# One more slot on the seven-product scheme, wider row maxima and a reordered list in a quantised GLU kernel

## The chip, the core and the metric

The kernel runs on one core of a Trainium2 chip. The metric is the device time of one execution in microseconds. The core's engines run side by side, each through its own list of instructions in order, and wait for each other on semaphores: TensorE (PE: matrix products into PSUM; PEld is its weight load), VectorE (DVE), ScalarE (ACT), GpSimd (POOL) and SyncE (SP), whose queue issues nearly all DMA transfers here. An instruction that waits holds up everything behind it on its engine or queue.

## The reference

Inputs are x (4 batches of 1024 tokens, 512 wide), a condition vector of 128 for each batch, and three weight matrices. Cut to what matters:

```python
scale = cond @ norm_w.T + 1.0
h = x * (scale[:, None, :] * rsqrt(mean(x * x) + EPS))
u = h @ up_w.T                        # 512 -> 4096
val, gate = split(u, 2)               # 2048 each
h = val * gelu(gate)
hq = round(h * 127 / max|h| per token) / (127 / max|h| per token)
wq = sign-like rounding of down_w by its mean magnitude
y = hq @ wq.T + x                     # 2048 -> 512
```

All four batches share the weights. The first projection is made in parts of fp16 (a high part and what is left of it), three matmul terms for each product, so that it holds fp32 accuracy.

## The kernel before

The 2048 columns of val and of gate are cut into NJ = 16 groups of 128, called slots; a global slot number g is batch times 16 plus j. A batch's 1024 tokens are two halves of 512. So a slot is a 2 by 2 arrangement of blocks (gate and val, each for two token halves), with the width of 512 split in two halves as well.

A slot can be made in two ways.

- *Plain* (function `plain`, matmuls at L705): four blocks, `gate.j.h` and `value.j.h` for h = 0, 1, each of twelve matmuls of 128x512 (four parts of the width, three terms). ACT then takes a gelu (`gelu.j.h`, L751) and DVE multiplies value and gelu (`out.j.h`, L761).
- *Seven products* (class `Slot`, matmuls at L690): a scheme of Strassen's kind over the 2 by 2 blocks. Seven products of six matmuls each are added up in three PSUM banks, with copies from bank to bank by ACT (L797, L805, L812), two gelus (L819, L836) and four DVE steps (L825, L833, L842, L845). Its operands are sums and differences of the weight blocks and of the token blocks.

Batches 1 to 3 make all slots by seven products, from weight sums that the first batch has spilled to DRAM (`s_spill`, L462) and that are loaded back (`s_load`, L476 and L478). In the first batch the weights themselves are still being read, scaled to powers of two, split, summed and transposed while PE works. There slots 0 to FAST - 1 are plain and slots FAST to 15 are made by seven products; FAST is NJ - 2 = 14.

What a slot j of the first batch needs, by the names of its steps: `w_load` (the two weight rows, 512 KB, L299), `w_range` (ACT, L315), `w_factor` (small DVE steps, L325 to L335), `w_scale` (ACT, L365), `rows_high` and `rows_low` (ACT L391, DVE L395: the high and low halves in fp16), `rows_turn` (a DMA transpose, L399, into the slot's place); and for the sums `s_sum` (four additions on POOL or DVE, L429), `s_high` (ACT, L446), `s_low` (POOL or DVE, L450) and `s_spill`. A slot on seven products in this batch also has its sums transposed on the spot by `s_turn` (two DMA transposes, L468) from `s_rows`, a pair of buffers that the next such slot uses again; its `rows_turn` moves three blocks out of four. The transposed weights lie in three places in turn (j modulo 3): two halves of SXY and an area of R. Batch 1's first slot, g = 16, uses the half of SXY that slot 13 had, and slot 17 that of slot 15.

The token side of batch 1 is made ready during batch 0 too: `t_load`, `t_square`, `t_root`, `t_scale`, `t_sum`, `t_high`, `t_low` and `t_turn` (a DMA transpose of 28 blocks, L665) for each of four groups of tokens. The quantised second weight is fetched and rounded by `d_fetch`, `d_round` and `d_sign`.

Row maxima for the quantisation: `pair_max` reduces a pair of neighbouring slots (128x1024 into 128x512, absolute maximum, L896; L891 for the first pair, straight into the result) and then combines the result with the maximum so far (L898). Step `max.i.h.n` is part n of the pair that begins at slot 2i. Pair 7 is left to batch 1.

The order of all these steps is written out by hand in `FIRST_BATCH`, one list for all engines: `take` calls each step in turn, and each puts its instructions at the end of its engine's list. In a step name the last number of `s_sum.j.n.1`, `s_low.j.n.1` and `t_sum.a.n.1` puts it on DVE; without it the step goes to POOL. `slot.g.k` is step k of a seven-product slot: 0, 2, 4, 6, 8, 10 and 13 are its products, 1, 3, 5, 7 and 12 are on ACT, 9, 11, 14 and 15 on DVE. PSUM banks are used in turn: a plain `value` uses one of two banks, which the `out` two values earlier must have read, and a `gate` one that a `gelu` must have read.

Of the kernel before, what the change touches and what calls it, by code (L numbers as in the profile page):

```python
# [51 lines left out]
def glu_quant_kernel(  # L52
# [90 lines left out]
    FAST = NJ - 2  # L143
# [742 lines left out]
    def pair_max(b, i, h):  # L886

        v = h_slots(b * NJ + 2 * i, 2)[:, :, h].rearrange("p j t -> p t j")
        m = m_view(b, h)
# [4 lines left out]
        def largest():
            gm.append(wpool.tile([P, TOK], F32, name=f"gm_{b}_{i}_{h}", tag="gm", bufs=1))
            DVE.tensor_reduce(gm[0], v, AX.X, ALU.max, apply_absolute_value=True)  # L896

        return [largest, lambda: DVE.tensor_tensor(m, m, gm[0], ALU.max)]  # L898
# [451 lines left out]
    def take(steps):  # L1350
# [15 lines left out]
        d_sum.7 c_range s_spill.1.0 rows_high.4 s_sum.2.3 d_load.1 s_spill.2.1 value.2.1 w_scale.5.0
        w_gain.2 o_sum.1 gelu.2.0 out.2.0 o_high.1 rows_low.4 rows_turn.4 gelu.2.1 gate.3.0 rows_high.5
        o_low.1 s_high.2.0 o_sum.2 s_high.2.1 value.3.0 o_sum.3 o_high.2 w_load.6 o_high.3 rows_low.5
        rows_turn.5 gelu.3.0 gate.3.1 out.2.1 d_sum.2 o_low.3 d_sum.3 max.0.0.0 s_spill.3.1 t_square.0.1
        value.3.1 d_sum.0 o_low.2 w_range.6 t_root.0 s_low.2.0.1 s_spill.2.0 c_spread d_sum.1 c_rows  # L1370
        gate.4.0 w_load.7 w_factor.6 s_sum.3.0 s_spill.4.1 w_scale.6.0 out.3.0 w_load.11 o_high.0 s_low.2.1
        s_spill.2.2 s_sum.3.1.1 w_scale.6.1 o_low.0 value.4.0 gelu.3.1 rows_high.6 out.3.1 s_sum.3.2.1
        s_sum.3.3 w_range.7 max.1.0.0 gate.4.1 w_load.8 s_high.3.1 rows_low.6 rows_turn.6 gelu.4.0
        s_high.3.0 s_low.3.0 c_copy s_low.3.1.1 w_factor.7 w_scale.7.1 value.4.1 max.0.1.0 w_scale.7.0
        t_load.1 out.4.0 s_sum.4.0 rows_high.7 rows_low.7 rows_turn.7 gelu.4.1 gate.5.0 w_range.8
        s_sum.4.1.1 d_total s_sum.4.2.1 s_sum.4.3.1 out.4.1 value.5.0 s_high.4.0 s_low.4.0 w_factor.8
        c_store w_scale.8.1 c_load c_undo w_scale.8.0 w_gain.6 d_spread gelu.5.0 s_sum.5.1.1 gate.5.1
        max.1.0.1 rows_high.8 s_sum.5.0.1 s_spill.5.1 s_sum.5.2.1 s_spill.3.2 w_range.9 out.5.0 s_spill.6.1
        rows_low.8 s_spill.3.0 value.5.1 s_spill.7.1 s_high.4.1 s_low.4.1 s_high.5.0 rows_turn.8 max.1.1.0
        gelu.5.1 c_bring max.1.1.1 gate.6.0 s_low.5.0.1 s_sum.6.1 s_sum.5.3.1 s_high.5.1 s_spill.5.0  # L1380
        w_factor.9 s_low.5.1 value.6.0 d_mean w_scale.9.1 s_sum.6.0.1 w_scale.9.0 t_scale.0.1 w_gain.8
        out.5.1 t_high.0.1 rows_high.9 t_sum.0.0.1 t_scale.0.0 gate.6.1 s_sum.6.2.1 t_high.0.0 t_sum.0.1
        max.2.0.0 gelu.6.0 s_spill.8.1 s_sum.6.3 s_high.6.0 t_low.0.0 w_range.10 value.6.1 rows_low.9
        rows_turn.9 gelu.6.1 t_sum.0.2.1 w_factor.10 w_scale.10.1 t_sum.0.3 s_low.6.0.1 gate.7.0 t_high.0.2
        t_low.0.1 out.6.0 w_scale.10.0 t_low.0.2 rows_high.10 s_spill.4.0 s_spill.5.2 value.7.0 s_sum.7.1.1
# [5 lines left out]
        w_scale.11.1 gate.8.1 gelu.8.0 s_spill.7.0 s_sum.9.0.1 out.7.1 s_sum.9.2.1 s_sum.9.1.1 s_high.9.0
        value.8.1 s_sum.9.3.1 w_load.12 t_sum.1.0.1 s_low.9.0.1 s_spill.8.2 rows_high.11 w_range.12
        rows_low.11 rows_turn.11 gate.9.0 max.3.0.1 out.8.0 t_scale.1.0 s_spill.9.0 value.9.0 gelu.8.1
        t_sum.1.1 t_load.2 gelu.9.0 w_factor.12 s_spill.11.1 out.8.1 w_scale.12.1 w_scale.12.0 s_sum.10.0.1
        t_sum.1.2.1 s_high.9.1 s_sum.10.1.1 gate.9.1 rows_high.12 t_sum.1.3 max.3.1.0 s_spill.7.2 s_low.9.1
        t_high.1.2 s_sum.10.2.1 max.3.1.1 t_high.1.1 s_high.10.0 s_sum.10.3.1 w_load.13 value.9.1
        rows_low.12 t_high.1.0 rows_turn.12 s_high.10.1 t_low.1.1 t_low.1.0 gelu.9.1 t_low.1.2 w_range.13
        gate.10.0 out.9.0 s_low.10.0.1 s_sum.11.0 t_turn.1 gelu.10.0 max.4.0.0 value.10.0 s_low.10.1 out.9.1
        s_spill.10.1 s_sum.11.2.1 s_sum.11.1.1 s_high.11.0 gate.10.1 max.4.0.1 s_sum.11.3.1 t_square.2.1
        s_low.11.0.1 s_sum.12.0 s_spill.12.1 s_high.11.1 w_load.14 gelu.10.1 w_factor.13 s_spill.11.0  # L1400
# [413 lines left out]
```

## Time and profile before

| what | us |
|---|---|
| median of 3 runs (723.93 to 724.92) | 723.95 |
| the profiled execution | 724.24 |
| its span, first to last instruction | 722.5 |
| PE busy | 716.2 |
| DVE busy | 584.4 |
| ACT busy | 420.0 |
| POOL busy | 139.4 |

A row of the profile in order of time has the start, the duration, the engine, the source line, the operation, the tile written and the tiles read, the shape and the number of merged instructions; brackets at its end hold the idle time before it and what released it. A grouped row has the count, then the busy time and the mean duration in ns, then the idle time before and its releasers. SPq stands for the queue of SP: its duration is the issuing of a transfer, not its landing.

### The profile page before, as it was taken

What the parts mean: (1) busy time and instruction counts of PE and PEld (TensorE: products, weight loads), DVE (VectorE), ACT (ScalarE), POOL (GpSimd) and SP (SyncE); (2) the same over time, 40 slices, a digit from 0 to 9 for tenths busy, and PEclk for the clock granted to TensorE, in tenths of its full rate; (3) what the DMA queues carried; (4) which work ended last, traced back from release to release, by engine and by line L of the source; (5) the groups of instructions that cost most, each with busy time, mean ns of one, the idle gap of its engine ahead of it and who ended that gap; (6) DMA issues with size and microseconds to landing.
All of it is one profiled execution on the core that took longest, in us unless ns stands there. A gap on an engine that the chain in (4) does not pass through costs nothing.

```text
span 722.5 us, 10223 instructions
## 1 busy us (share of the span) xinstructions
PE 716.2 (99%) x3676; PEld 360.7 (50%) x3676; DVE 584.4 (81%) x876; ACT 420.0 (58%) x697; POOL 139.4 (19%) x143
## 2 busy tenths in 40 slices
PE   8999999999999999999999999999999999999998
PEld 4544444444444446665444445665444444445854
DVE  7888799784898899787689887677678888755896
ACT  6898776765667774553335676544433665333473
POOL 1634331322100124440100030360020000000120
PEclk9999999999999999999999999999999999999999
DMA  7799889989995765877845646765965455453253
GB/s 276 258 290 266 236 199 254 288 185 243 281 205 117 132 157 130 210 169 176 167 101 103 131 102 184 189 162 160 216 93 111 101 103 101 102 100 98 103 172 121
DMA packets 228405, 122.64 MB, mean 170 GB/s; under 512 B 189801, under 2 KB 199805, under 8 KB 228354
## 3 DMA queue, kind: packets, MB, share of 16 engines
q1 hardware_dynamic: 228202, 121.85, 69.1%
q8 instruction: 29, 0.48, 0.3%
q14 instruction: 22, 0.18, 0.1%
q10 hardware_dynamic: 152, 0.13, 0.1%
HBM read 53.50 MB, written 23.09 MB: 106 GB/s over the span
## 4 chain that ended last, share of the span: by engine, by line
PE 96%; DVE 2%; DMA 1%; ACT 1%; SPq 0%; issue 0%
PE A L690 34%; PE E L690 17%; PE pg L705 10%; PE pv L705 10%; PE po L1052 9%; PE B L690 9%; PE po_end L1004 4%; DMA SXY<-s_rows 1%; PE pz L1169 1%; DVE gm L896 1%; PE ptx L1153 1%; PE pv L776 0%; PE po_B L1052 0%; DVE R L898 0%; PE pg L776 0%; DVE R L891 0%
## 5 line engine op out<-in xcount | busy, mean ns | idle before, releaser
L690 PEld LDWEIGHTS <-SXY 128*128 128x128 f16 x2058 | 201.2, 98 | 236.5 <-DMA SXY<-s_rows 0.7
L690 PE MATMUL A<-R,SXY 128*128 128x512 f16 x1158 | 267.4, 379 | 0.0
L690 PE MATMUL E<-R,SXY 128*128 128x512 f16 x582 | 141.4, 379 | 0.1
L825 DVE SCALAR_TENSOR_TENSOR H<-A,sg,t 128x512 f32<-128x512 f32 x50 | 37.5, 750 | 72.6 <-PE A L690 72.4
L976 DVE TENSOR_TENSOR H<-H,am 128x1024 f32<-128x1024 f32 x64 | 76.1, 1214 | 0.0
L836 ACT ACTIVATE t<-t,sg 128x512 f32<-128x512 f32 x50 | 36.0, 721 | 64.8 <-DVE t L833 64.7
L690 PE MATMUL B<-R,SXY 128*128 128x512 f16 x294 | 71.4, 379 | 0.0
L896 DVE TENSOR_REDUCE gm<-H 128x512 f32<-128x1024 f32 x56 | 69.1, 1233 | 0.9
L705 PEld LDWEIGHTS <-SXY 128*128 128x128 f16 x438 | 42.8, 98 | 51.6 <-DVE SXY L417 0.4
L912 POOL PARTITION_ALL_REDUCE am<-R x8 | 14.4, 1795 | 229.4 <-DVE R L898 229.4
L819 ACT ACTIVATE t<-B,sg 128x512 f32<-128x512 f32 x50 | 34.4, 688 | 38.3 <-PE B L690 38.3
L1052 PE MATMUL po<-wd,R 128*128 128x256 fp8e4 x416 | 52.4, 273 | 0.0
L705 PE MATMUL pg<-R,SXY 128*128 128x512 f16 x228 | 52.4, 379 | 0.0
L812 ACT COPY t<-A 128x512 f32<-128x512 f32 x50 | 29.0, 581 | 35.5 <-PE A L690 35.2
L705 PE MATMUL pv<-R,SXY 128*128 128x512 f16 x210 | 48.9, 379 | 0.0
L1052 PEld LDWEIGHTS <-R 128*128 128x128 bf16 (+1 forms) x448 | 43.8, 98 | 8.9
L805 ACT COPY v<-E 128x512 f32<-128x512 f32 x50 | 29.3, 586 | 31.6 <-PE E L690 28.0
L797 ACT COPY B<-A 128x512 f32<-128x512 f32 x50 | 28.6, 572 | 30.5 <-PE A L690 29.9
L845 DVE SCALAR_TENSOR_TENSOR H<-v,sg,t 128x512 f32<-128x512 f32 x50 | 38.8, 776 | 7.6 <-ACT t L836 7.6
L984 ACT ACTIVATE H<-H 128x1024 f32<-128x1024 f32 x38 | 39.9, 1050 | 5.2 <-DVE H L976 5.2
L842 DVE TENSOR_TENSOR v<-A,v 128x512 f32<-128x512 f32 x50 | 34.1, 683 | 10.7 <-PE A L690 9.6
L898 DVE TENSOR_TENSOR R<-R,gm 128x512 f32<-128x512 f32 x56 | 40.6, 725 | 1.0
(237 smaller groups left out, 932.5 us busy)
## 6 DMA issues: line engine op xcount, KB each, us to landing
SXY<-s_dram SPq DMA_DIRECT2D x48, 256.0 KB, 3.2
H<-in_L_cond_up_w_dram SPq DMA_DIRECT2D x13, 512.0 KB, 5.0
s_dram<-SXY SPq DMA_DIRECT2D x17, 384.0 KB, 3.2
SXY<-s_dram SPq DMA_DIRECT2D x48, 128.0 KB, 3.3
xr<-in_x_dram SPq DMA_DIRECT2D x19, 256.0 KB, 3.2
out_dram<-xr SPq DMA_DIRECT2D x19, 256.0 KB, 2.8
H<-in_x_dram SPq DMA_DIRECT2D x8, 512.0 KB, 5.8
R<-in_L_cond_down_w_dram SPq DMA_DIRECT2D x8, 512.0 KB, 6.7
```

Source lines behind the costliest of these rows:

```text
L690: PE.matmul(o, s[:, w, k, :], operand(g // NJ, c, l, k), start=start and n == 0, stop=stop and n == len(TERMS) - 1, skip_group_check=True,)
L705: PE.matmul(ps, a[k // 2][:, w, k % 2, :], XP[:, l, k, h * TOK : (h + 1) * TOK], start=n == 0, stop=n == len(terms) - 1,)
L819: ACT.activation(self.t1, self.B, AF.Gelu, scale=gain(self.g, 1))
L825: DVE.scalar_tensor_tensor(h_half(self.g, 0), self.A, gain(self.g, 0), self.t1, ALU.mult, ALU.mult)
L836: ACT.activation(self.t2, self.t2, AF.Gelu, scale=gain(self.g, 1))
L842: DVE.tensor_tensor(self.v, self.A, self.v, ALU.add)
L845: DVE.scalar_tensor_tensor(h_half(self.g, 1), self.v, gain(self.g, 0), self.t2, ALU.mult, ALU.mult)
L896: DVE.tensor_reduce(gm[0], v, AX.X, ALU.max, apply_absolute_value=True)
L898: return [largest, lambda: DVE.tensor_tensor(m, m, gm[0], ALU.max)]
L976: DVE.tensor_tensor(v, v, r.to_broadcast([P, 2, TOK]), ALU.mult)
L984: ACT.activation(v, v, AF.Copy, bias=MAGIC)
L1052: PE.matmul(po, w[:, j], m, start=start and j == 0, stop=stop and j == n - 1, skip_group_check=True,)
```

## The change

FAST goes from 14 to 13, so slot 13 of the first batch is made by seven products; `pair_max` takes a number of slots, and the first batch reduces slots 0 to 3, 4 to 7 and 8 to 11 at once (the steps `max.1`, `max.3` and `max.5` go) and the pair 12, 13 as before; the list is reordered from its first line on. In that list nine additions (six `s_sum`, three `t_sum`) and one of the `s_low` go from POOL to DVE. The diff, with the list cut to its end:

```diff
-    FAST = NJ - 2
+    FAST = NJ - 3
...
-    def pair_max(b, i, h):
-
-        v = h_slots(b * NJ + 2 * i, 2)[:, :, h].rearrange("p j t -> p t j")
+    def pair_max(b, i, h, n=2):
+
+        v = h_slots(b * NJ + 2 * i, n)[:, :, h].rearrange("p j t -> p t j")
...
     def lm(i, h, n):
         if n == 0:
-            made["m", i, h] = pair_max(0, i, h)
+            made["m", i, h] = pair_max(0, i, h, 2 if i == 6 else 4)
...
     FIRST_BATCH = """
...
-        s_high.15.0 s_low.15.0 t_sum.3.0.1 s_turn.14.1 t_sum.3.2.1 t_sum.3.3.1 s_spill.13.1 t_high.3.2
-        t_low.3.2 value.13.1 s_spill.15.1 gelu.13.1 gelu.13.0 s_turn.15.0 s_sum.15.3 out.13.0 slot.14.0
-        slot.14.1 t_low.3.1 s_spill.14.2 s_sum.15.1 slot.14.2 t_low.3.0 t_turn.3 max.5.0.1 out.13.1
-        slot.14.4 gains slot.14.6 slot.14.5 s_high.15.1 s_low.15.1 slot.14.3 slot.14.13 slot.14.14 slot.14.7
-        d_fetch.1 slot.15.0 slot.15.1 s_spill.15.0 s_load.16.0 s_turn.15.1 slot.15.2 s_load.16.1 slot.15.6
-        slot.15.7 d_fetch.2 slot.14.8 slot.14.9 d_fetch.3 s_spill.15.2 s_load.16.2 d_round.1 s_load.17.0
-        slot.15.4 s_spill.12.2 max.5.1.0 slot.14.10 slot.15.5 d_sign.0 max.5.1.1 slot.15.13 s_load.17.1
-        slot.14.11 d_sign.1 slot.14.12 slot.14.15 slot.15.3 s_spill.14.1 max.6.0.0 d_fetch.5 s_load.16.3
-        slot.15.14 max.6.0.1 d_fetch.4 s_spill.13.2 max.6.1.0 max.6.1.1
...
+        s_sum.13.2.1 gelu.11.1 out.11.1 t_root.3 rows_high.14 gate.12.0 s_high.13.0 out.11.0 w_gain.14
+        s_high.12.1 s_low.13.0 s_low.12.1.1 w_load.15 s_turn.13.0 value.12.0 s_sum.13.3.1 s_sum.14.0.1
+        s_high.13.1 max.4.0.0 gelu.12.0 s_low.13.1 gate.12.1 s_sum.14.1 s_turn.13.1 rows_low.14 w_range.15
+        s_spill.13.0 s_sum.14.2 s_spill.13.2 d_fetch.0 value.12.1 w_factor.15 rows_turn.14 gelu.12.1
+        out.12.0 w_scale.15.0 t_scale.3.0 s_high.14.0 s_low.14.0 s_turn.14.0 s_sum.15.0.1 slot.13.0
+        w_scale.15.1 slot.13.2 slot.13.1 s_sum.14.3 rows_high.15 t_scale.3.1 slot.13.4 s_high.14.1
+        s_spill.11.2 t_high.3.0 s_low.14.1.1 s_spill.14.2 slot.13.6 t_sum.3.1.1 slot.13.5 out.12.1
+        s_spill.14.0 d_round.0 s_turn.14.1 t_sum.3.0.1 slot.13.13 gains rows_low.15 slot.13.7 rows_turn.15
+        w_gain.15 s_sum.15.1.1 slot.14.0 slot.13.3 s_sum.15.2.1 t_low.3.0 slot.14.1 s_sum.15.3 slot.13.14
+        slot.14.2 t_sum.3.2.1 s_spill.13.1 s_high.15.0 s_low.15.0.1 t_sum.3.3 t_high.3.1 slot.14.6
+        s_high.15.1 s_low.15.1 t_high.3.2 t_low.3.1 s_spill.15.0 s_turn.15.0 slot.13.8 t_low.3.2 s_turn.15.1
+        slot.14.4 slot.13.9 d_fetch.1 slot.13.10 slot.14.5 t_turn.3 slot.14.3 slot.14.7 slot.14.13
+        slot.13.11 max.4.0.1 slot.15.0 slot.15.1 slot.14.14 max.4.1.0 slot.15.2 s_load.16.0 d_sign.0
+        s_load.16.1 slot.15.6 slot.15.7 s_spill.15.1 slot.14.8 slot.14.9 d_fetch.2 s_spill.15.2 slot.13.12
+        d_fetch.3 slot.15.4 d_round.1 slot.13.15 slot.14.10 slot.15.5 s_load.16.3 slot.15.3 d_sign.1
+        slot.15.13 slot.14.11 s_load.17.0 slot.15.14 slot.14.12 slot.14.15 max.4.1.1 s_load.17.1 max.6.0.0
+        s_load.16.2 max.6.0.1 s_spill.14.1 d_fetch.5 max.6.1.0 max.6.1.1 d_fetch.4 s_spill.12.2
     """
```

Earlier in the list, what the prediction speaks of stands so before and after:

```diff
-        s_high.1.0 s_low.0.1.1 s_spill.0.0 s_sum.1.3 gate.2.0 w_factor.4 w_range.5 w_load.10 out.0.1
-        rows_turn.3 w_scale.4.1 w_factor.5 s_high.1.1 out.1.1 value.2.0 d_sum.5 s_low.1.1 w_scale.5.1
...
-        gate.8.0 out.7.0 max.3.0.0 s_spill.6.0 w_scale.11.0 s_spill.6.2 value.8.0 s_spill.9.1 w_gain.10
...
+        gelu.1.1 value.1.1 s_sum.1.0.1 s_sum.1.2.1 s_high.0.1 out.1.1 t_square.0.0 s_low.0.1 s_spill.0.0
+        w_range.5 s_sum.1.3 d_load.0 gate.2.0 d_sum.5 o_sum.0 d_sum.6 s_sum.1.1.1 w_load.10 out.0.1
+        s_high.1.0 value.2.0 rows_turn.3 c_largest w_factor.4 d_sum.7 w_factor.5 w_gain.2 s_high.1.1
...
+        rows_turn.10 out.7.0 gate.8.0 s_sum.8.0.1 max.2.0.0 gelu.7.1 s_sum.8.1 s_spill.6.0 s_spill.7.0
+        value.8.0 s_spill.6.2 s_sum.8.2.1 s_high.8.0 out.7.1 s_sum.8.3.1 w_scale.11.1 s_low.8.0.1
```

More of the change, by code (lines that the diff above doesn't have):

```diff
@@ L1366, in glu_quant_kernel @@
[L1366 to L1385, printed above, removed]
@@ L1391, in glu_quant_kernel @@
[L1391 to L1400, printed above, removed]
@@ new lines, in glu_quant_kernel @@
+        s_low.1.0.1 w_scale.4.0 c_over w_scale.4.1 gate.2.1 s_sum.2.1.1 s_sum.2.0.1 w_scale.5.1 s_low.1.1.1
+        s_spill.1.0 o_sum.1 rows_high.4 d_load.1 s_spill.2.1 w_scale.5.0 s_sum.2.2.1 rows_low.4 rows_turn.4
+        value.2.1 o_high.1 s_sum.2.3 c_range gelu.2.0 o_high.3 out.2.0 gate.3.0 s_high.2.1 d_sum.2 o_sum.2
+        rows_high.5 o_sum.3 w_gain.4 gelu.2.1 value.3.0 o_low.1 d_sum.3 w_load.6 out.2.1 s_high.2.0
+        rows_low.5 rows_turn.5 gelu.3.0 gate.3.1 o_high.2 o_low.3 d_sum.0 o_low.2 w_range.6 w_load.11
@@ new lines, in glu_quant_kernel @@
+        s_spill.8.0 s_high.8.1 gate.8.1 s_low.8.1.1 t_scale.1.0 s_spill.8.2 s_sum.9.0.1 s_spill.9.1
+        s_sum.9.1.1 s_sum.9.2.1 s_high.9.0 s_low.9.0 t_sum.1.0.1 s_sum.9.3.1 w_load.12 value.8.1
+        rows_high.11 rows_low.11 rows_turn.11 gelu.8.0 gelu.8.1 w_range.12 gate.9.0 max.2.0.1 out.8.0
+        out.8.1 s_high.9.1 t_sum.1.1.1 t_load.2 value.9.0 s_sum.10.1.1 s_spill.9.0 w_factor.12 s_spill.11.1
+        s_sum.10.0.1 w_scale.12.0 t_sum.1.2.1 gelu.9.0 max.2.1.0 t_sum.1.3 w_scale.12.1 s_low.9.1 gate.9.1
@@ new lines, in glu_quant_kernel @@
+        t_high.1.1 rows_high.12 s_sum.10.2 s_spill.7.2 max.2.1.1 s_high.10.0 s_sum.10.3.1 w_load.13
+        t_high.1.2 rows_low.12 value.9.1 s_spill.9.2 t_high.1.0 rows_turn.12 out.9.0 gelu.9.1 t_low.1.1
+        s_high.10.1 s_low.10.1 t_low.1.0 gate.10.0 t_low.1.2 t_square.2.1 out.9.1 t_turn.1 s_low.10.0.1
+        t_square.2.0 value.10.0 gelu.10.0 t_root.2 s_sum.11.0.1 w_range.13 s_sum.11.2.1 s_sum.11.1
+        s_high.11.0 gate.10.1 w_factor.13 s_sum.11.3 s_low.11.0.1 w_gain.12 w_load.14 w_scale.13.0
@@ new lines, in glu_quant_kernel @@
+        s_spill.11.0 s_sum.12.0.1 t_scale.2.1 s_spill.12.1 value.10.1 gelu.10.1 s_spill.10.1 t_sum.2.0.1
+        t_load.3 w_scale.13.1 t_scale.2.0 s_spill.10.0 rows_high.13 t_sum.2.1.1 out.10.0 s_high.11.1
+        w_range.14 gate.11.0 s_sum.12.1.1 s_low.11.1 t_sum.2.2.1 t_sum.2.3.1 rows_low.13 rows_turn.13
+        t_high.2.0 value.11.0 s_sum.12.2.1 t_high.2.2 out.10.1 t_high.2.1 s_high.12.0 s_low.12.0 t_low.2.1
+        w_factor.14 gelu.11.0 t_low.2.0 gate.11.1 w_scale.14.1 s_spill.12.0 w_scale.14.0 s_spill.10.2
```

50 lines of the change are left out of this document (25 added, 25 removed).

## The prediction

> **What bounds the kernel now.** I read the page first, then busy time by stretches, then PE in order of time, then what held PE, and last the neighbours (DVE, ACT, POOL, the DMA queue of SP) at those places.
>
> ```profile
> span 722.5 us, 10223 instructions
> ...
> PE 716.2 (99%) x3676; PEld 360.7 (50%) x3676; DVE 584.4 (81%) x876; ACT 420.0 (58%) x697; POOL 139.4 (19%) x143
> ...
> 0.00:20.00 20.00, 17.30 (x85) 9.38 (x86) 16.17 (x77) 13.23 (x30) 4.12 (x9) 1.00 0.74 255
> ...
> 60.00:80.00 20.00, 20.00 (x96) 9.24 (x94) 14.27 (x32) 16.26 (x31) 6.62 (x7) 1.00 0.91 230
> 80.00:100.00 20.00, 20.00 (x94) 8.98 (x92) 19.83 (x36) 15.14 (x32) 5.40 (x7) 1.00 0.83 224
> 100.00:120.00 20.00, 20.00 (x93) 8.99 (x92) 18.95 (x36) 13.53 (x25) 7.41 (x10) 1.00 0.97 250
> ...
> 160.00:180.00 20.00, 19.76 (x93) 8.84 (x91) 9.79 (x15) 11.25 (x17) 5.05 (x5) 1.00 1.07 247
> ...
> 700.00:723.00 23.00, 19.21 (x105) 10.09 (x103) 16.60 (x24) 10.30 (x10) 0.00 (x0) 1.00 0.46 157
> ```
>
> The columns behind each stretch are PE, PEld, DVE, ACT and POOL, then the granted clock, the DMA share and GB/s. PE is busy for all but 6.3 us of the span, and nearly all of that lies in the first 20 us (2.70) and the last 23 (3.79), which the change does not touch. So the time is the number of matmuls times their pitch, plus short waits. The clock is 1.00 throughout. DVE is a near second in the first batch: 38.8 of the 40 us from 80 to 120.
>
> ```profile
> 83.33 2.75 PE L705 MATMUL pv<-R,SXY 128*128 128x512 f16 x12
> 85.99 2.75 PE L705 MATMUL pg<-R,SXY 128*128 128x512 f16 x12
> ...
> 98.94 2.75 PE L705 MATMUL pv<-R,SXY 128*128 128x512 f16 x12
> 101.68 2.75 PE L705 MATMUL pg<-R 128*128 128x512 f16 x12
> 104.38 2.75 PE L705 MATMUL pv<-R 128*128 128x512 f16 x12
> ...
> 161.35 2.75 PE L705 MATMUL pv<-R,SXY 128*128 128x512 f16 x12
> 163.94 1.46 PE L690 MATMUL A<-R 128*128 128x512 f16 x6
> ...
> 176.90 1.46 PE L690 MATMUL E<-R 128*128 128x512 f16 x6
> 178.59 1.47 PE L690 MATMUL A<-wd,SXY 128*128 128x512 f16 x6 [0.24 <-DMA SXY<-s_rows]
> 179.90 1.46 PE L690 MATMUL A<-R,SXY 128*128 128x512 f16 x6
> ```
>
> Starts tell more than durations, whose ends are modelled. Twelve matmuls take 163.94 - 161.35 = 2.59 us, so one takes 0.216 us and a product of six 1.295. Against this pitch PE loses 0.07 (85.99), 0.15 (101.68), 0.11 (104.38) and 0.395 us (178.59, due at 178.195): 0.725 us of waits in the first batch.
>
> ```profile
> 96.41 0.73 DVE L761 SCALAR_TENSOR_TENSOR H<-g,sg,pv 128x512 f32<-128x512 f32 x1
> ...
> 100.95 0.68 ACT L751 ACTIVATE g<-pg,sg 128x512 f32<-128x512 f32 x1
> ...
> 103.59 0.74 DVE L761 SCALAR_TENSOR_TENSOR H<-g,sg,pv 128x512 f32<-128x512 f32 x1
> ...
> 166.69 4.17 SPq L665 DMA_TRANSPOSE R<-nx  x1
> ...
> 172.69 5.85 DMA SXY<-s_rows
> ```
>
> The wait at 101.68 ends with ACT's gelu.7.0 (100.95 + 0.68), which frees the bank of gate.8.0; the one at 104.38 with DVE's out.7.0 (103.59 + 0.74), which frees that of value.8.0. The one at 178.59 ends when s_turn.15.1 lands (the last row is from the chain); it was issued only at 172.69, because t_turn.3 held SP's queue for 4.17 us and three more transfers stood in between. The out at 96.41 is out.6.1, used below.
>
> **The change, part by part.** Its own sum is made on the profiled execution: 724.24 us (span 722.5 and 1.74 around it), 0.29 above the median of 723.95; what is gained there I take off the median.
>
> *Products.* Slot 13 of batch 0 loses 4 plain blocks of 12 matmuls and gets 7 products of 6: 48 becomes 42, and the built programs differ by six matmuls. On the path: 6 x 0.216 = -1.295 us. Nothing else of PE changes.
>
> *The tail of the list.* s_turn.15.1 moves ahead of d_fetch.1, t_turn.3 and s_load.16.0. Between its place and slot.15.13, which needs it, stood 5 products (6.5 us); now there are 9 (11.7 us). It took 5.85 us, so the 0.395 us goes: -0.395. What is late next is t_turn.3, all of whose output slot 16's first product reads: 8 products follow its place (10.4 us) where 10 did (13.0).
>
> ```profile
> R<-nx SPq DMA_TRANSPOSE x8, 6.6
> ...
> SXY<-H SPq DMA_TRANSPOSE x9, 4.4
> ...
> s_dram<-s_rows SPq DMA_DIRECT2D x4, 256.0 KB, 3.6
> ...
> 43.45 2.33 SPq L399 DMA_TRANSPOSE SXY<-H  x1
> ...
> 49.01 1.24 PE L705 MATMUL pg<-R,SXY 128*128 128x512 f16 x5
> ```
>
> With 6.6 us to land it has 3.8 to spare: 0. If the queue ahead (s_turn.15.1, d_fetch.1) holds it for more, each us is PE's. s_load.16.1 keeps its 5 products of lead. Slot 13's own two transposes are listed 9.1 and 7.8 us ahead of need, against 4.4 for a longer one: 0. The smaller row transposes of slots 14 and 15 keep 6.5 and 9.1 us (10.4 and 11.7 before): 0. s_rows has two buffers, so s_high.14.0 waits on ACT for the spill of slot 13 (3.6 us to land); behind it stands slot 13's first copy, which PE wants two products later. Between 0 and about 1 us on ACT; I take 0 on PE.
>
> *The early list.* All other moves are in the same plan of PE; I compare leads. Row transposes of slots 4 to 13 stand 13 us or more ahead of their gates, that of slot 2 as far as before (5.2). Only one shrinks to where it could matter: rows_turn.3, whose place moves from 7.9 to 5.3 us ahead of gate.3.0. It was in fact issued at 43.45, held by the landing of s_spill.0.0, with 5.56 us to gate.3.0 at 49.01: 1.2 above the median landing. It still stands behind that spill; d_load.0 (512 KB, formerly ahead of the spill) now stands between. Bytes ahead are the same: 0; at worst the 2.1 us that 512 KB takes at 250 GB/s (the stretch 100 to 120 above), less 1.2: +0.9. At best the earlier spill gives nothing, since PE does not wait there.
>
> *DVE, ACT and POOL.*
>
> ```profile
> L896 DVE TENSOR_REDUCE gm<-H 128x512 f32<-128x1024 f32 x12 | 14.8, 1231 | 0.1
> L395 DVE TENSOR_TENSOR H<-H 128x1024 f16<-128x1024 f32 x12 | 14.6, 1218 | 2.3 <-ACT H L391 2.2
> ...
> L898 DVE TENSOR_TENSOR R<-R,gm 128x512 f32<-128x512 f32 x12 | 8.2, 684 | 0.1
> ...
> L450 DVE TENSOR_TENSOR SXY<-H,SXY 128x768 f16<-128x768 f32 x6 | 6.4, 1061 | 0.2 <-ACT SXY L446 0.2
> ...
> L395 DVE TENSOR_TENSOR H<-H 128x768 f16<-128x768 f32 x2 | 1.9, 951 | 0.0
> ...
> L429 DVE TENSOR_TENSOR H<-H x39: 405/416/779, 33.1 to 159.4; 128x256 f32<-128x256 f32 x39
> L429 POOL TENSOR_TENSOR H<-H x25: 724/732/1713, 20.4 to 165.0; 128x256 f32<-128x256 f32 x25
> ...
> L761 DVE SCALAR_TENSOR_TENSOR H<-g,sg,pv 128x512 f32<-128x512 f32 x23 | 17.0, 738 | 1.8 <-PE pv L705 1.3 <-ACT g L751 0.4
> ...
> L842 DVE TENSOR_TENSOR v<-A,v 128x512 f32<-128x512 f32 x2 | 1.4, 686 | 2.7 <-PE A L690 2.7
> ...
> L751 ACT ACTIVATE g<-pg,sg 128x512 f32<-128x512 f32 x27 | 18.1, 680 | 5.3 <-PE pg L705 5.1
> ...
> L797 ACT COPY B<-A 128x512 f32<-128x512 f32 x3 | 1.7, 570 | 3.5 <-PE A L690 3.5
> ```
>
> A maximum over four slots is not in the trace. Its ends are one two-slot reduce (1.23) and two (2.46); L395's two sizes give (1.218 - 0.951)/256 = 1.04 ns per element, so 1.23 + 1024 x 1.04 ns = 2.30, near the upper end. Fourteen reduces and twelve combinations become six of 2.30, two of 1.23 and six combinations: -12 x 1.231 - 6 x 0.684 + 6 x 2.30 = -5.1 us of DVE.
>
> [...]
>
> Back come six s_sum and three t_sum moved from POOL (9 x 0.42 = +3.8), one s_low from POOL (+1.0), slot 13's four results, two like L842 and two like L761, for two outs (+1.4), and 0.27 less for its rows: +0.8 us net in the 158 us of the batch. ACT gets three copies (0.57) and two gelus for two gelus: +1.7. POOL loses ten instructions of 0.73 us and more. None of this is on PE's path by itself; what covers it is the lead of each out, which frees a bank for PE. I summed DVE's list up to each out with these durations, less 0.08 us by which neighbours overlap. Ahead of out.6.1 it grows by 2.0 us, of out.7.0 (where PE waited) by 0.0, of out.7.1 by -0.6, of out.8.0 by 1.2, of out.9.0 by -0.9. Where DVE had idle time earlier (5.7 us from 60 to 80) the 2.0 can go; so I leave the small waits as they are: 0, ends -0.33 (all gone) and +2.0.
>
> *Sum:* -1.295 - 0.395 = -1.69; 723.95 - 1.69 = 722.26, by the profiled execution 722.55. I predict 722.3.
>
> **Rivals.**
> 1. *Only the matmuls are won.* t_turn.3 or a slot 13 transpose takes the place of s_turn.15.1 as PE's last wait, of about the same size. For it: DMA share 1.07 in 160 to 180 and two transposes more. Against: 3.8 us to spare. -1.295: 722.65.
> 2. *All waits go.* Shorter maxima and an emptier POOL let DVE reach out.7.0 in time: -1.295 - 0.725 = -2.02, 721.93. For it: L429 on DVE takes 779 ns at worst against 416, when POOL is at work. Against: DVE's list there is no shorter. [...]
> 3. *Slower: DVE falls behind between 75 and 130 us.* The first batch's DVE is full there; a four-slot reduce in front of an out holds it 1.1 us longer than a two-slot one, the list has 2.0 us more ahead of out.6.1, and value.7.1 started 1.8 us after that out had ended (98.94 against 97.14). Every us of lag that no idle time takes is PE's, and ten values follow. It eats the gain at 1.7 us of lag, and is seen as slower from 3.1. Two four-slot reduces in the wrong place and the 2.0 us make 2 x 1.1 + 2.0 = 4.2 us, net +2.5: 726.5. Against: a list that fills DVE so closely lost only 0.33 there.
> 4. *Nothing:* new waits of 1.3 to 2 us in several places: 724.
>
> **How the numbers follow.** Forecast 0.42, rival 1 0.18, rival 2 0.12, rival 3 0.20, rival 4 0.08. 0.2% (1.45 us) is about what a measurement tells from no change, so 722.50 is the bound: the forecast lies just beyond it (-0.23%) and gives 0.40 to faster and 0.02 to same; rival 2 is faster, rival 1 within, rival 3 slower; rival 4 gives 0.06 to same and 0.02 to slower. Faster 0.52, same 0.26, slower 0.22. The range reaches from below rival 2 to where rival 3 decides: 721.7 to 725.3. The forecast's own range is 721.9 to 722.7.
>
> **What would show it.** PE's matmuls 3670. In order of time, slot 13's first product at about 153.6 us, in place of its first plain block (the plan of PE up to there is unchanged); slot 16's first at 178.2 instead of 179.90. No wait of PE on s_rows; the four-slot reduces at 2.3 us. Wrong would be: a wait of PE on R<-nx before slot 16, on DVE's outs from 90 to 130 us, or gate.3.0 later than 49.0.

## The result and the profile after

The changed kernel takes 727.21 us (median of 6 runs, 725.50 to 727.89), the kernel before 723.94 us on the same chip (6 runs, 723.76 to 724.92): ratio 1.0040, 95% interval 1.0027 to 1.0053. So it is slower by 3.3 us, where 722.3 was forecast.

The profiled execution of the changed kernel took 725.50 us. Its page, and busy time by stretches (columns as in the prediction):

```profile
span 723.7 us, 10197 instructions
...
PE 714.9 (99%) x3670; PEld 360.0 (50%) x3670; DVE 593.5 (82%) x876; ACT 421.5 (58%) x700; POOL 125.6 (17%) x133
```

```profile
60.00:80.00 20.00, 20.00 (x96) 9.21 (x95) 18.64 (x33) 18.31 (x37) 2.56 (x5) 1.00 0.85 237
...
100.00:120.00 20.00, 18.52 (x87) 8.30 (x86) 18.76 (x28) 10.38 (x20) 4.70 (x6) 1.00 0.82 235
...
160.00:180.00 20.00, 19.59 (x91) 8.73 (x90) 15.04 (x21) 12.92 (x21) 3.32 (x4) 1.00 1.06 252
```

PE has its six matmuls less (3670) and its clock is 1.00 as before. DVE is busy 9.1 us longer (593.5 against 584.4), although it has as many instructions (876); from 60 to 80 us it went from 14.27 to 18.64. PE, which had lost nothing between 105 and 178 us, now loses 1.5 us between 100 and 120. PE in order of time shows where:

```profile
109.06 2.75 PE L705 MATMUL pv<-R 128*128 128x512 f16 x12
113.30 2.75 PE L705 MATMUL pg<-R,SXY 128*128 128x512 f16 x12 [1.49 <-ACT g L751]
...
154.74 1.46 PE L690 MATMUL A<-R,SXY 128*128 128x512 f16 x6
156.03 1.46 PE L690 MATMUL E<-wd,SXY 128*128 128x512 f16 x6
157.44 1.46 PE L690 MATMUL A<-wd,SXY 128*128 128x512 f16 x6
...
160.03 1.46 PE L690 MATMUL A<-wd,SXY 128*128 128x512 f16 x6
161.90 1.47 PE L690 MATMUL A<-R 128*128 128x512 f16 x6 [0.41 <-DMA R<-H]
...
178.74 1.46 PE L690 MATMUL A<-wd,SXY 128*128 128x512 f16 x6
180.04 1.46 PE L690 MATMUL A<-R,SXY 128*128 128x512 f16 x6
...
213.71 1.46 PE L690 MATMUL E<-R,SXY 128*128 128x512 f16 x6
216.26 2.75 PE L690 MATMUL A<-R,SXY 128*128 128x512 f16 x12 [1.09 <-ACT t L812]
```

Against the pitch (2.59 us for twelve, 1.295 for six) PE is late by 1.65 us at gate.9.0 (113.30), 0.11 at 157.44, 0.57 at slot 14's first product (161.90) and 1.25 in batch 1's slot 20 (216.26): 3.58 us, where it had been 0.725. So waits cost 2.86 us more, the products save 1.295, and 1.56 is left; the two profiled executions differ by 725.50 - 724.24 = 1.26. This execution is the shortest of its six; the others are 1.4 to 2.4 us longer.

What made gate.9.0 late is read from DVE and ACT in order of time:

```profile
102.85 3.71 DVE L896 TENSOR_REDUCE gm<-H 128x512 f32<-128x2048 f32 x1
106.48 0.41 DVE L429 TENSOR_TENSOR H<-H 128x256 f32<-128x256 f32 x1
...
109.77 1.09 DVE L429 TENSOR_TENSOR H<-H 128x256 f32<-128x256 f32 x3
```

```profile
106.98 0.83 ACT L446 CAST R<-H 128x768 f16<-128x768 f32 x1 [3.15 <-issue]
...
110.89 0.83 ACT L446 CAST SXY<-H 128x768 f16<-128x768 f32 x1 [2.16 <-DVE H L429]
111.62 1.04 ACT L391 CAST H<-H 128x1024 f16<-128x1024 f32 x1
112.57 1.26 ACT L751 ACTIVATE g<-pg,sg 128x512 f32<-128x512 f32 x2
```

The wide reduce max.2.0.0 takes 3.71 us, not 2.30. The sums of slots 8 and 9 (s_sum, L429) stand behind it on DVE, and s_high.8.0 and s_high.9.0 on ACT stand idle before they start (3.15 and 2.16 us). For the second the profile names the sum. For the first it names nothing ("issue"); that it waits for the sum is inferred, since it starts 0.09 us after s_sum.8.2 has ended on DVE (106.48 + 0.41), while POOL's last sum for it had ended at 104.67. gelu.8.0 stands behind both on ACT, and it frees gate.9.0's bank at about 113.2 us. All six wide reduces of the changed kernel are as long (grouped by form, 20 to 185 us):

```profile
L896 DVE TENSOR_REDUCE gm<-H 128x512 f32<-128x2048 f32 x4 | 14.9, 3732 | 0.0
...
L891 DVE TENSOR_REDUCE R<-H 128x512 f32<-128x2048 f32 x2 | 7.5, 3750 | 0.0
```

### The profile page after: what moved, and what is told of

The parts are those of the page before. It is cut to its first block, busy times and chain, and to the rows that moved or that the text cites. A ratio compares the mean times of both kernels' runs of the same rounds, so it can differ in the third digit from the quotient of the medians.

```text
span 723.7 us, 10197 instructions
## 1 busy us (share of the span) xinstructions
PE 714.9 (99%) x3670; PEld 360.0 (50%) x3670; DVE 593.5 (82%) x876; ACT 421.5 (58%) x700; POOL 125.6 (17%) x133
## 4 chain that ended last, share of the span: by engine, by line
PE 85%; DVE 6%; DMA 4%; ACT 3%; issue 2%; SPq 0%; POOL 0%; DVEq 0%; POOLq 0%; ACTq 0%
PE A L690 34%; PE E L690 17%; PE po L1052 9%; PE B L690 8%; PE pg L705 5%; PE pv L705 5%; PE po_end L1004 4%; DMA dn<-in_L_cond_down_w_dram 2%; DMA R<-H 1%; DVE R L891 1%; PE pz L1169 1%; DVE H L395 1%; DMA H<-in_L_cond_up_w_dram 1%; DVE H L761 1%; DVE gm L896 1%
## 5 line engine op out<-in xcount | busy, mean ns | idle before, releaser
L690 PE MATMUL E<-R,SXY 128*128 128x512 f16 x588 | 142.9, 379 | 0.1
L690 PE MATMUL B<-R,SXY 128*128 128x512 f16 x300 | 72.9, 379 | 0.0
L896 DVE TENSOR_REDUCE gm<-H 128x512 f32<-128x1024 f32 (+1 forms) x50 | 71.6, 1433 | 0.9
L812 ACT COPY t<-A 128x512 f32<-128x512 f32 x51 | 29.6, 580 | 35.7 <-PE A L690 34.9
L705 PE MATMUL pg<-R,SXY 128*128 128x512 f16 x204 | 46.8, 379 | 1.5 <-ACT g L751 1.5
L797 ACT COPY B<-A 128x512 f32<-128x512 f32 x51 | 29.2, 572 | 32.2 <-PE A L690 31.7
L705 PE MATMUL pv<-R,SXY 128*128 128x512 f16 x186 | 43.4, 379 | 0.0
L833 DVE TENSOR_TENSOR t<-E,t 128x512 f32<-128x512 f32 x51 | 34.6, 677 | 7.5 <-PE E L690 7.3
```

The source lines that it names most:

```text
L690: PE.matmul(o, s[:, w, k, :], operand(g // NJ, c, l, k), start=start and n == 0, stop=stop and n == len(TERMS) - 1, skip_group_check=True,)
L705: PE.matmul(ps, a[k // 2][:, w, k % 2, :], XP[:, l, k, h * TOK : (h + 1) * TOK], start=n == 0, stop=n == len(terms) - 1,)
L833: DVE.tensor_tensor(self.t2, self.E, self.t2, ALU.add)
```

## The experiments

Theory: the wide reduce was mis-priced, and everything that is lost follows from DVE being held longer. Rivals: the reordered list or slot 13's new scheme costs the time by itself; or batch 1's start does. Each kernel is compared with the kernel before on the same chip (median 723.55 to 723.66 there).

**The changed kernel once more** (no edit).

> The changed kernel once more, for a second profile: the recorded one (725.50 us) was the shortest of six executions, whose median was 727.21. If the waits of the recorded profile are the whole story (gate.9.0 1.65 us late, slot 14's first product 0.58, slot 20's 1.26), they stand here too, and the 1.7 us between 725.5 and 727.2 shows as one more wait or a longer one. If the waits wander from run to run, DMA is behind them; if those at gate.9.0 and slot 14 stay to 0.1 us, an engine's fixed work is.

725.87 us in one execution. Late again at gate.9.0 (0.94) and at slot 14's first product (0.45); in batch 1 the waits on ACT's L812 came at 196.81 (0.61) and 216.62 (1.68). A wait of 0.38 us at slot 13's third product (156.88, released by ACT's L797) was 0.11 in the first profile. The waits at gate.9.0 and at slot 14 belong to the kernel, but not with a fixed size: gate.9.0 was due 0.12 us earlier here (111.53 against 111.65) and started 0.83 us earlier (112.47 against 113.30). The waits of batch 1 change place from one execution to the next.

**The reduce alone.** The whole computation is left out; DVE reduces 512 columns over 2, 3, 4 and 8 slots (rows 4096 bytes apart), over rows 2048 and 2064 bytes apart, and over 2 and 4 neighbouring elements, four times each.

```diff
+    S = H.rearrange("p (s h) t -> p s h t", h=2)
+    v = S[:, 0:4, 0].rearrange("p j t -> p t j")
+    DVE.tensor_reduce(m, v, AX.X, ALU.max, apply_absolute_value=True)
```

> Leaves out the whole computation: it loads x, runs ten forms of the absolute-maximum reduce four times each and stores x and one maximum. Order: two, three, four and eight neighbouring slots (rows 4096 bytes apart), two and four rows 2048 bytes apart, two and four elements that lie side by side, two and four rows 2064 bytes apart. Theory 'width': the reduce pays for each input row that it walks in turn once there are more than two; four, eight rows cost about 1.8 ns an element at any distance, two rows and side by side 1.05 to 1.2. Theory 'distance': rows a power of two apart collide, and 2064 bytes apart four rows take 2.3 us. My prediction had 2.3 us for four slots.

Grouped by form, one window for each (2, 3, 4 and 8 slots; 4 neighbours; 4 rows 2064 bytes apart):

```profile
L68 DVE TENSOR_REDUCE m<-H 128x512 f32<-128x1024 f32 x4 | 4.9, 1230 | 25.3 <-DMA H<-in_x_dram 25.2
...
L68 DVE TENSOR_REDUCE m<-H 128x512 f32<-128x1536 f32 x4 | 7.7, 1912 | 0.1
...
L68 DVE TENSOR_REDUCE m<-H 128x512 f32<-128x2048 f32 x4 | 14.5, 3618 | 0.1
...
L68 DVE TENSOR_REDUCE m<-H 128x512 f32<-128x4096 f32 x4 | 28.1, 7032 | 0.1
...
L68 DVE TENSOR_REDUCE m<-H 128x512 f32<-128x2048 f32 x4 | 9.1, 2286 | 0.1
...
L68 DVE TENSOR_REDUCE m<-H 128x512 f32<-128x2048 f32 x4 | 14.5, 3620 | 0.1
```

2048 elements take 2.29 us when the four of one maximum lie side by side, and 3.62 us when they come from four rows. Two rows cost nothing extra (1230 ns; two neighbours 1220), three little (1.24 ns an element), four 1.77 and eight 1.72. Rows 2048, 2064 or 4096 bytes apart cost the same (two rows 1.23 us, four 3.62), so theory 'distance' falls. In these ten forms the price of an element differs with the number of rows that are walked in turn and not with how far apart the rows are; distances between neighbours and 2048 bytes were not measured.

**Pairs in place.** Each wide reduce becomes two reduces over pairs, in the same place of the list.

```diff
-            made["m", i, h] = pair_max(0, i, h, 2 if i == 6 else 4)
...
+            first, second = pair_max(0, i, h), pair_max(0, i + 1, h)
+            made["m", i, h] = [lambda: [f() for f in [*first, second[0]]], second[1]]
...
```

> The changed kernel with each four-slot reduce made of two two-slot reduces and one more combination at the same place of the list: 1.23 + 0.68 + 1.23 less overlaps = 3.0 us of DVE in place of 3.7. Theory 'reduce' (the four-slot reduce is what makes DVE late): gate.9.0 comes 0.7 us earlier, slot 14's first product on time, 726.0 us in the median. Theory 'list' (the waits come from the order and from the DMA traffic of slot 13's transposes): 727.2, as before.

725.44 us, ratio 1.0034 (1.0017 to 1.0052): no gain over the changed kernel (1.0027 to 1.0053) that the intervals show, and no choice between the two expectations. DVE is held for 3.6 us in one place here too (two reduces of 1.23 and a combination of 1.16), and gate.9.0 was late by 1.76 us, gate.5.0 by 1.32. Undoing the width without undoing the places does not help.

**Few maxima.** The maxima of slots 2 to 11 of batch 0 are left out of the changed list, all else stays; the output's scale then rests on the other slots.

```diff
-        max.2.0.0 max.2.0.1 max.2.1.0 max.2.1.1 ... max.4.0.0 max.4.0.1 max.4.1.0 max.4.1.1
...
-            made["m", i, h] = pair_max(0, i, h, 2 if i == 6 else 4)
+            made["m", i, h] = pair_max(0, i, h, 2)
```

> The changed kernel without the maxima of slots 2 to 11 of the first batch (only slots 0, 1, 12 to 15 are reduced, so the first batch's quantisation is wrong); everything else stands in the same order. DVE loses some 22 us. Theory 'reduce': the waits at gate.9.0 and at slot 14's first product go, 725.0 us or less; with the wait at slot 20 gone too, 721.9. Theory 'list': they stay, 726.5 to 727.2.

721.96 us, ratio 0.9979 (0.9969 to 0.9989). The reordered list and the new slot 13 without that DVE work are faster than before: the loss needs the maxima, and the moves alone do not make it. The profiled execution was an unusually long one (726.09) with a wait of 2.51 us on ACT's L812 in batch 1, so that wait does not need the maxima. The twelve matmuls behind it took 4.27 us in place of 2.59, at a granted clock of 0.83 (195 to 205 us, with 1.00 in the ten us on either side). In the kernel before, the changed kernel's two executions and pairs in place the clock was 1.00 from 165 to 225 us; why it fell here is open.

**Wide reduces in the list of before.** The old list, slot 13 plain; `max.0`, `max.2` and `max.4` reduce four slots at the places of the second pairs, `max.1`, `max.3` and `max.5` go.

```diff
-            made["m", i, h] = pair_max(0, i, h)
+            made["m", i, h] = pair_max(0, i, h, 2 if i == 6 else 4)
...
```

> The list of before with slot 13 plain, and only the maxima changed: reduces over four slots (slots 0 to 3, 4 to 7, 8 to 11) at the places of the second pair of each four; the first pair's steps go. Theory 'hold' (a wide reduce holds VectorE 3.7 us in one piece, 2.5 us more than a pair, and what is listed behind it frees TensorE's banks too late): slower than before by 0.5 to 3 us, 724.5 to 727, with TensorE late at a gate or value behind such a reduce between 75 and 130 us. Rival 'moves' (the wide reduces are harmless in a list that was not reordered, and the loss after the change comes from the other moves): within 0.3 us of before.

734.06 us, ratio 1.0143 (1.0128 to 1.0159): slower by 10.5 us, far more than expected. PE in order of time, the late starts (3.50, 0.91, 2.02 and 2.31 us against the pitch):

```profile
88.92 2.75 PE L705 MATMUL pg<-R,SXY 128*128 128x512 f16 x12 [3.34 <-DVE wmean L525]
...
113.14 2.75 PE L705 MATMUL pv<-R 128*128 128x512 f16 x12 [0.75 <-DVE H L761]
...
130.70 2.75 PE L705 MATMUL pv<-R,SXY 128*128 128x512 f16 x12 [1.86 <-DVE H L761]
...
173.15 1.46 PE L690 MATMUL E<-wd,R 128*128 128x512 f16 x6 [2.15 <-DVE H L761]
```

All are releases by DVE. Put where the second pairs stood, the wide reduces alone do the damage of rival 3, so 'moves' falls. The changed list has the same reduces and lost 3.58 us to waits.

**Pairs spread.** In the changed list the maxima of slots 2 to 11 are taken over pairs, each at a place where DVE was idle with few maxima, all after 115 us.

```diff
-        max.2.0.0 ... max.4.1.1
+        out.8.1 max.1.0.0 ... value.9.0 max.1.0.1 ... out.9.0 max.1.1.0 max.1.1.1 ... out.9.1 max.2.0.0
+        max.2.0.1 ... out.10.0 max.2.1.0 max.2.1.1 ... out.10.1 max.3.0.0 max.3.0.1 ...
```

> The changed kernel with maxima over pairs, each pair's reduce and combination moved to a place where VectorE had idle time when the maxima were left out (all of slots 2 to 11 from 115 us on). Nothing else moves. Theory 'hold': the waits at gate.9.0 and at slot 14's first product go; 1.65 + 0.57 us less than the changed kernel's profile, ratio to before 0.998 to 1.001. Rival 'fullness' (the same VectorE work costs the same wherever it stands in the first batch): as with pairs in place, ratio 1.002 to 1.004.

728.57 us, ratio 1.0069 (1.0045 to 1.0093): the worst version of the changed list but one, and both expectations missed. gate.9.0 and slot 14 were in time or nearly so; PE waited instead for outs behind the added pairs:

```profile
135.50 2.75 PE L705 MATMUL pv<-R 128*128 128x512 f16 x12 [0.55 <-DVE H L761]
...
148.18 2.75 PE L705 MATMUL pv<-R,SXY 128*128 128x512 f16 x12 [2.16 <-DVE H L761]
```

Idle time summed over ten microseconds was no guide: what counts is what stands ahead of each out.

**Fetches earlier.** The changed kernel with two of the second weight's fetches moved up in SP's queue; the wide reduces stay.

```diff
-        s_load.17.0 ... s_load.17.1 ... s_spill.14.1 d_fetch.5 max.6.1.0 max.6.1.1 d_fetch.4 s_spill.12.2
+        d_fetch.4 s_load.17.0 ... d_fetch.5 s_load.17.1 ... s_spill.14.1 max.6.1.0 max.6.1.1 s_spill.12.2
```

> The changed kernel with d_fetch.4 and d_fetch.5 moved from the end of the list to ahead of s_load.17.0 and s_load.17.1; the wide maxima stay. Theory 'queue' (in batch 1 ScalarE waits for the second weight's fetch, issued at 188.13 instead of 185.70 and 187.42 us while TensorE runs 1.3 us ahead, and the bank copy of L812 that TensorE needs is queued behind that wait): TensorE's waits on ScalarE's L812 at 197 and 216 us go, 1.2 to 2.3 us off the changed kernel's median, ratio to before 1.001 to 1.0025; gate.9.0 stays late. Rival 'bandwidth' (what is late in batch 1 is late because the DMA engines are full, wherever a transfer stands): ratio 1.003 to 1.005, the waits only shift to another transfer.

726.97 us, ratio 1.0043 (1.0030 to 1.0055), as the changed kernel. The waits on L812 are gone, and two on the weight sums' loads have come (1.36 and 1.38 us against the pitch):

```profile
190.55 1.47 PE L690 MATMUL A<-R,SXY 128*128 128x512 f16 x6 [1.20 <-DMA SXY<-s_dram]
...
193.24 1.47 PE L690 MATMUL E<-R,SXY 128*128 128x512 f16 x6 [1.22 <-DMA SXY<-s_dram]
```

The ratio and the shift of the waits are what the rival 'bandwidth' forecast. That a different order of these transfers only chooses who waits is read from this one profile, and whether bandwidth or the issuing on one queue sets it isn't told apart.

**Both edits.** The diffs of the last two, together.

> Both edits at once: pairs moved to idle places, d_fetch.4 and d_fetch.5 earlier. Theories 'hold' and 'queue' together: TensorE loses less than 0.7 us to waits in the first 230 us; ratio to before 0.9975 to 0.9985, faster than both kernels. If either falls, 0.999 to 1.002.

730.30 us, ratio 1.0088 (1.0075 to 1.0101), beyond both expectations: the waits of both kernels, one after the other (2.32 us at 148.63, 1.53 and 1.44 at 193.55 and 196.30).

**The wide reduce at the predicted price.** The same reduces, on the same slots, in the same places, but over four neighbours.

```diff
+        if n == 4:
+            v = h_slots(b * NJ + 2 * i, n)[:, :, h].rearrange("p j (t k) -> p j t k", k=4)
...
```

> The changed kernel with its four-slot reduces reading the same slots, in the same places, but four neighbouring elements at a time instead of one from each slot, which took 2.29 us in the measurement of the reduce alone: the price that the prediction had. The maxima are then of neighbours and not of slots, so the computation is another in that part; every wait and every transfer is the same. Theory 'price' (the prediction's one failed term is the reduce's duration, 2.30 instead of 3.73 us): TensorE late at gate.9.0 by 0.3 us at most, ratio to before 0.997 to 0.9985. Rival 'place' (the list stands in the way even at that price: pairs spread over idle time lost more than the wide reduces): ratio 1.001 to 1.004.

722.00 us, ratio 0.9975 (0.9965 to 0.9985). With this one duration as forecast the time is as forecast: 1.66 us less than before on this chip, where 1.69 was predicted. The reduce takes 2.28 us, DVE is busy 586.2 us, and gate.9.0 starts on its pitch. DVE, ACT and PE of this kernel, to be laid beside the rows of the changed kernel above:

```profile
100.63 2.28 DVE L900 TENSOR_REDUCE gm<-H 128x512 f32<-128x2048 f32 x1
...
106.44 1.09 DVE L429 TENSOR_TENSOR H<-H 128x256 f32<-128x256 f32 x3
```

```profile
107.56 0.83 ACT L446 CAST SXY<-H 128x768 f16<-128x768 f32 x1 [2.16 <-DVE H L429]
...
109.25 1.26 ACT L751 ACTIVATE g<-pg,sg 128x512 f32<-128x512 f32 x2
```

```profile
108.61 2.75 PE L705 MATMUL pv<-R 128*128 128x512 f16 x12
111.20 2.75 PE L705 MATMUL pg<-R,SXY 128*128 128x512 f16 x12
```

gelu.8.0 now ends at about 109.9 us, 1.3 us before gate.9.0 is due; in the changed kernel it ended 1.6 us after. The sums of slot 9 come 3.33 us earlier (106.44 against 109.77). This reduce itself is 1.43 us shorter, and it starts 2.22 us earlier, since two wide reduces that stand ahead of it on DVE are cheaper as well and PE is 0.45 us earlier; one sum behind it took 0.33 us longer. PE has no wait at all from 60 to 260 us in this execution, in batch 1 neither, with the same list for SP. The medians say that the price cost more than the first profile's waits show: the ratios differ by 0.0065, which is 4.7 us. But how DVE would bring the waits of batch 1 is not shown: one profile without the wide maxima had such a wait (few maxima), and one with DVE as busy as in the changed kernel from 165 to 225 us (49.99 us against 49.81) had none (pairs in place).

**One wide reduce later.** max.2.0.0 moves behind gate.9.0, nothing else.

```diff
-        ... s_sum.8.0.1 max.2.0.0 gelu.7.1 ... gate.9.0 max.2.0.1 out.8.0
+        ... s_sum.8.0.1 gelu.7.1 ... gate.9.0 max.2.0.0 max.2.0.1 out.8.0
```

> The changed kernel with one step moved: the wide reduce max.2.0.0 from behind s_sum.8.0.1 to just ahead of its own combination, behind gate.9.0 (about 9 us later). Theory 'hold': gate.9.0 is late by 0.4 us at most, since gelu.8.0 on ScalarE no longer stands behind a sum that waits for the reduce; the 3.7 us now stand ahead of out.8.0, so the value after next may be late instead by 0 to 1.5 us; ratio to before 1.000 to 1.004. If gate.9.0 is as late as it was (0.9 to 1.7 us), the reduce is not what holds it.

727.37 us, ratio 1.0055 (1.0042 to 1.0067). gate.9.0 is in time (111.25), so it is late only with that reduce ahead of it; and value.9.0, which needs the bank that out.8.0 reads, is late by 3.37 us, more than expected. The reduce and out.8.0 on DVE, then PE:

```profile
112.10 3.67 DVE L896 TENSOR_REDUCE gm<-H 128x512 f32<-128x2048 f32 x1
115.81 0.69 DVE L898 TENSOR_TENSOR R<-R,gm 128x512 f32<-128x512 f32 x1
116.42 1.40 DVE L761 SCALAR_TENSOR_TENSOR H<-g,sg,pv 128x512 f32<-128x512 f32 x2
```

```profile
111.25 2.75 PE L705 MATMUL pg<-R,SXY 128*128 128x512 f16 x12
117.21 2.75 PE L705 MATMUL pv<-R,SXY 128*128 128x512 f16 x12 [3.21 <-DVE H L761]
```

**The early list of before, the late list of the change.** The list of before up to gate.10.1, then the changed one with slot 13 by seven products; pairs throughout.

```diff
-    FAST = NJ - 2
+    FAST = NJ - 3
...
-        ... gate.10.1 max.4.0.1 s_sum.11.3.1 t_square.2.1 ... (list of before)
+        ... gate.10.1 max.4.0.1 s_spill.9.2 t_square.2.1 ... (changed list; max.4.1 and max.5 over pairs)
```

> The list of before up to gate.10.1 (about 125 us), then the changed list with slot 13 by seven products; maxima over pairs throughout, those of slots 8 to 11 at 145 to 180 us. Theory 'early list' (what the change loses is lost by VectorE's fuller list up to 125 us, and the products are won): 1.3 to 1.7 us less than before, ratio 0.9975 to 0.9985, faster than both kernels. Rival 'tail' (slot 13 by seven products itself costs waits of about the size of the matmuls that it saves, as pairs_spread showed at 148 and from 159 to 168 us): ratio 0.999 to 1.003.

723.58 us, ratio 0.9996 (0.9987 to 1.0005): outside the range of 'early list' and inside that of 'tail', but not by the waits that 'tail' named. Its profiled execution (724.52, the second longest of eleven) has no wait above 0.13 us up to 187 us, and slot 16's first product starts at 177.81, 2.09 us earlier than before: the products and the small waits are won by then. Then come 0.46 us on SXY<-s_dram and 2.01 at 197.14 on ACT's L812, which stood behind a fetch of the second weight:

```profile
195.47 1.15 ACT L543 ACTIVATE dn<-dn,wsc 128x1024 f32<-128x1024 f32 x1 [2.24 <-DMA dn<-in_L_cond_down_w_dram]
196.52 0.57 ACT L812 COPY t<-A 128x512 f32<-128x512 f32 x1
```

So the gain can also be given back at batch 1's start. The transpose that loads weight sums (L476) ahead of that fetch took SP's queue 4.89 us here and 3.56 with the reduces as priced; why they differ stays open.

**Threes.** The maxima over three slots (0 to 2, 3 to 5, 6 to 8, 9 to 11) and a pair, the added steps ahead of w_factor.13, 14 and 15.

```diff
-        v = h_slots(b * NJ + 2 * i, n)[:, :, h].rearrange("p j t -> p t j")
...
+        v = h_slots(b * NJ + at * i, n)[:, :, h].rearrange("p j t -> p t j")
...
-            made["m", i, h] = pair_max(0, i, h, 2 if i == 6 else 4)
+            made["m", i, h] = pair_max(0, i, h, 2 if i == 12 else 3, 1)
...
```

> The changed kernel with the row maxima taken over three slots at once (0 to 2, 3 to 5, 6 to 8, 9 to 11) and the pair 12, 13: a reduce over three took 1.91 us alone against 3.62 over four. Slots 0 to 2 and 3 to 5 stand where the first two fours stood; those of slots 6 to 8 and 9 to 11 go to gaps that VectorE had with the reduces as priced (before w_factor.13, w_factor.14 and w_factor.15, and the places of the third four). Theory 'price': ahead of each out up to 125 us VectorE has no more to do than with the reduces as priced, so TensorE's waits stay below 0.7 us and the ratio to before is 0.997 to 0.999, faster than both kernels. Rival 'place': as with pairs_spread, an out between 125 and 150 us comes late behind the added triples, ratio 1.000 to 1.004.

722.57 us, ratio 0.9987 (0.9977 to 0.9997): faster than both kernels, with the full computation, by 1.0 us against the kernel before. The steps also stand at other places, so this run tests price and places together. PE's only wait above 0.1 us from 60 to 260 us is 0.48. A reduce over three takes 1.91 us in place:

```profile
L896 DVE TENSOR_REDUCE gm<-H 128x512 f32<-128x1536 f32 x6 | 11.5, 1908 | 0.0
```

## Why the prediction was wrong

- *The step that failed* is the price of the four-slot reduce: "1.23 + 1024 x 1.04 ns = 2.30, near the upper end", with two two-slot reduces (2.46) as the upper bound. It measured 3.73, above both ends. The bound assumed that a second pair of rows costs what the first did (alone, two rows took 1.23 us and four 3.62), and L395's slope came from rows that are read straight on. Six times 1.43 is 8.6 us of DVE. The forecast for DVE was +0.8 net and it came out at +9.1, so this term is all of the 8.3 us between them; with the reduce at 2.28 us DVE's busy time was 1.8 us above that of before. The forecast price is what four neighbours cost alone (2.286 us). Why four rows cost more, and two rows nothing extra (1.230 us against 1.220 for two neighbours), is not shown.
- *Most of the rest of the sum was right.* With the reduce at 2.28 us the gain is 1.66 us against 1.69. Matmuls 3670: right. The wait at s_turn.15.1: gone, right (178.74 and 180.04 are on the pitch). t_turn.3, the transposes of slot 13 and rows_turn.3: no wait, right. The term for s_rows, "I take 0 on PE": slot 13's first copy made PE wait 0.11 us (0.38 in the second profile), but ACT's list did not wait for s_rows; it ran nearly without a gap behind w_range.15, which had waited 3.06 us for w_load.15.
- *"I leave the small waits as they are: 0, ends -0.33 and +2.0"*: with the reduce as priced all of them went, which is rival 2's course; its runs cannot tell 721.9 from 722.3. An emptier POOL, which rival 2 gave as a reason, does not show: L429 on DVE took 425 ns in the mean before, 440 in the changed kernel and 447 with the reduces as priced. Before, the one of 779 ns ran beside POOL's L450, but the others that overlapped POOL took 406 to 429. As built, the waits on DVE and ACT were 1.65 at gate.9.0 and came through a path that the prediction had not followed: sums on DVE, copies on ACT, then the gelu behind them. It had looked at the outs only.
- *Slot 14's row transpose*, "keep 6.5 us": it was issued at 154.48 us, 6.85 us ahead of need, and took 7.4 us to land, so PE started 0.57 too late. The term that was short is the landing. Its rows were ready earlier: rows_low, which stood behind the wide reduce max.4.0.0, ended at 153.59, and the rows below show SP's queue at work without a gap up to the issue. That stretch begins with t_turn.2, issued 0.03 us after DVE's last step for it had ended (140.87 + 2.67), so it began late because DVE was late; this is inferred from the times. With the reduces as priced that step of DVE ended 3.2 us earlier (137.67 + 2.67) while PE was 2.1 us earlier (slot 13's first product at 152.65 against 154.74), and slot 14's first product started on its pitch (159.12).

```profile
152.64 0.95 DVE L395 TENSOR_TENSOR H<-H 128x768 f16<-128x768 f32 x1
```

```profile
143.57 4.41 SPq L665 DMA_TRANSPOSE R<-nx  x1
148.07 0.54 SPq L299 DMA_DIRECT2D H<-in_L_cond_up_w_dram  x1
148.70 4.07 SPq L468 DMA_TRANSPOSE SXY<-s_rows  x2
152.82 1.05 SPq L462 DMA_DIRECT2D s_dram<-s_rows  x2
153.91 0.46 SPq L539 DMA_DIRECT2D dn<-in_L_cond_down_w_dram  x1
154.48 1.66 SPq L399 DMA_TRANSPOSE R<-H  x1
```

- *Rival 3* is what happened in kind, at 0.20: DVE fell behind between 75 and 130 us. It counted 1.1 us for holding DVE with a wide reduce, where 2.5 was true (3.73 against 1.23), and 2.0 us of list ahead of out.6.1, where no value came late. That its size (726.5) is close to 727.21 is luck in part: of the 3.3 us lost, the first profile shows 1.56, and the only wait of that kind in it is the 1.65 at gate.9.0.
- *Not settled*: what the executions of 727 us lose beyond the profiled one. In two of them 0.6 and 0.8 us more than in the profiled one lie outside the span. The kernel with earlier fetches loses 2.7 us at batch 1's start, so the rest may be there.

## What to carry to other kernels

Before two reduces are merged, time the merged form on the access pattern that it will have: the cost of an element is not a property of the operation alone (1.12 ns here over four neighbours, 1.77 over four rows), and two small reduces are no upper bound (2.46 us against 3.62). On an engine that is nearly full (DVE here was busy for 18.76 of the 20 us from 100 to 120), price an edit by what stands ahead of each instruction that frees a bank or feeds another engine, and follow that through the other engine's list, and the transfer queue's, as well; idle time summed over a stretch says little. When a forecast fails, put the single doubtful duration right and leave all else: that run told more here than five that moved steps.

## What the runs showed of the hardware that was not expected

- The reduce's time by rows walked in turn, for 512 results in fp32: 1.23 us for two rows, 1.91 for three, 3.62 for four, 7.03 for eight; 2.29 for four neighbours. Rows 2048, 2064 or 4096 bytes apart cost the same (two rows 1.23 us, four 3.62). In the kernel, beside other engines, four rows took 3.73.
- The issue of the same transpose (L476, the third behind t_turn.3) held SP's queue for 3.12 to 4.89 us at the same place of the list. In eight profiles of kernels with the changed list's end, four had 4.25 us or more, and PE then waited 2.3 to 2.7 us between 185 and 222 us; in the four with 3.12 to 3.56 it waited 0 to 1.25 us. The two go together; which causes which isn't shown.
- With two transfers moved up in that queue the wait on ACT's L812 (1.25 us) was gone and two on SXY<-s_dram had come (1.36 and 1.38), in one profile of each kernel.
- One profile (few maxima) had a granted clock of 0.83 from 195 to 205 us, just behind a wait of 2.51 us, and 0.998 in the mean of its execution; in the executions with waits of 3.37 us (one wide reduce later) and 3.50 us (wide reduces in the list of before) the mean was 0.999 and 1.000.
